# The 3x3 convolution of an image moved into the next image's attention stretch, and its last norm and routing moved behind that image's Gelu

## The chip, the core and the metric

The kernel runs on one core of a Trainium2 chip. The metric is the device time in microseconds of one execution. The engines are PE (TensorE, matrix products), DVE (VectorE), ACT (ScalarE), POOL (GpSimd) and SP (SyncE, which issues most DMAs). Each takes its instructions in the order in which the program lists them, and an instruction that waits holds up all those behind it on its engine.

## The reference

Four images of 256 channels and 32 x 32 = 1024 positions, all in float32. Each image goes through a mixing network and then, as 1024 tokens, through a mixture of eight experts of which each token takes two:

```python
xm = mamba_v(xc, ...) + skip_scale * xc              # 4 selective scans over 1024 steps
g  = sigmoid(conv1d(conv1d(x_concat, ...)))          # gates
R  = conv1d(conv1d(xg, ...)) + xg                    # depthwise and pointwise
xm2 = conv1d(conv1d(cat, ...)) + cat[:, :C]
x_local  = conv1d(xm2, lc_w, ...)                    # depthwise
x_global = mha(xm2, ...)                             # 8 heads over 1024 positions
x_out = gelu(layernorm(concat(x_local, x_global) @ fc_w.T + fc_b))
xi = conv3x3_depthwise(ln_hw(x_out))                 # norm over positions, then 3 x 3
x  = x + layernorm(xi) @ proj_w.T + proj_b
# experts, per token
top_w, top_i = top_k(layernorm(t) @ Wg + bg, 2)
t = t + sum_of_two(softmax(top_w) * (gelu(t_n @ W1[e] + b1[e]) @ W2[e] + b2[e]))
```

## The kernel before, in words

**Work pieces.** Every piece of an image's work is a Python generator that emits instructions and yields a number of ticks. `scan(at, i, stop)` emits one step of the selective scan; an image has eight parts (four scans of two halves) of 16 steps. A step is, on DVE, the product dBu (L538, into PSUM) and the scan hs (L545); on ACT the decay dA (L531); on POOL hs times cs (L550) and, in first halves, a copy of the last column (L549); on PE the sums of states yp (L556) and the spread bs (L523). A part ends with `finish_part` or its like inside the next part: yp, the gather on DVE (L563), a product on POOL (L566), the output matmul op on PE (L571), the skip on DVE (L577).

**The order.** It is written by hand. `beat()` advances a tick and lets every running generator that is due emit its next instructions. The main loop calls one scan step and one beat in turn, so background pieces are laced between scan steps. For image b > 0:

- with part 0, `convolutions(b - 1)` starts (gates, depthwise and pointwise convolutions, then the values, queries and keys of attention);
- after part 3, `drain()` runs all background to its end, and the attention stretch begins: `attention(b - 1)` followed by `mixing(b - 1)`, `finish_part`, `local(b - 1)` (the depthwise convolution into xloc) and `normalised(b + 1)` (the first norm of the next image: mean and variance matmuls on PE, L343; DVE L396 and L418; POOL L406, L416, L421);
- no scan step is emitted until attention has three of its 32 steps left; then parts 4 to 7 of image b run, with the rest of attention and `mixing(b - 1)` in the background.

An attention step (`logits`, then the products with the values) is 4 products st on PE (L861), 4 exponentials on ACT (L871), 4 products av (L903); every second step DVE adds the exponentials in pairs (L913), which the sums with a matrix of ones on PE read a step later (L881). DVE scales a finished block (L893).

**`mixing(b)`** is one generator: the output product of attention (ao) and the joint product (fc), on PE with ACT evictions; a norm over channels (squares on ACT, `column_mean` on PE, `root` on ACT, a product on DVE, L987); Gelu (L993); then statistics over positions (L1005, L1006), the image normed and padded by windows (xz, L1022), the centre tap (L1027, ACT) and eight further taps per half of the channels on DVE (L1035: 16 an image); then the last norm (mean matmuls, centring L1045, squares, variance, root, product L987), the projection (pr, added to the input xr, L1062) and `experts.dispatch`: 16 transposes (raw, L1428), statistics (L1438), gate products, the two best experts, places by counts, and 16 indirect DMAs on POOL (L1539), each preceded by a memset (L1538), which scatter the rows to the experts' regions in DRAM.

**The tail.** After the last scan, `finish_part`, `convolutions(3)` and `tiles()` run together. `tiles()` multiplies blocks of 256 rows of one expert: SP loads the weights (2 MB) and the rows (xs), PE transposes the rows (xp, L1734), 16 products h (L1757) with Gelu on ACT (L1762), 16 products y (L1767), DVE adds the bias and weighs, POOL adds the rows to the output by indirect DMA (L1778). The tiles come in series of 8, 8 and 23, of which the last four are done only if needed: series 0 needs the rows of images 0 and 1, series 1 those of image 2, series 2 those of image 3. Tiles are held while `attention(3)` runs, and go on beside `mixing(3)`, at a rate that `PACE` sets. Last, `bring_back` transposes the result to the output.

**Buffers.** Tiles of an image's size lie in a pool of eight (`a8`), those of half that in a pool of seven (`a4`), rows of 512 in a pool of 17 (`a2`); PSUM has eight banks.

Of the kernel before, what the change touches and what calls it, by code (L numbers as in the profile page):

```python
# [16 lines left out]
NC2 = C // P  # L17
# [54 lines left out]
def network(  # L72
# [70 lines left out]
    with tc.tile_pool(name="w_conv", bufs=1) as wp, tc.tile_pool(  # L143
# [789 lines left out]
            del XM2[b]  # L933


        def mixing(b):

            xloc, oT = XLOC.pop(b), OT.pop(b)
            xglo = a8(f"xglo_{b}")

            def pace(ticks):

                if b == B - 1:
                    T["pace",] = ticks

            pace(PACE["product"])
            yield from in_turn(
                CO_H, lambda at: product(
                    f"ao_{b}_{at[0]}_{at[1]}", aoutT_s, at[0],
                    [oT[ci][:, half(at[1])] for ci in range(NC2)],  # L950
                ),
                lambda at, r: nc.scalar.activation(
                    xglo[:, at[0], half(at[1])], r, AF.Identity, bias=ob[:, at[0] : at[0] + 1]
                ),
            )

            xc = a8(f"xc_{b}")
            both = (xloc, xglo)
# [10 lines left out]
            def inverse_deviation(name):  # L969
                r = a4(f"r_{name}")  # L970

                def squares(h):
                    sq = [a2(f"sq_{name}_{h}_{c}") for c in range(NC2)]
                    for c in range(NC2):
                        nc.scalar.activation(sq[c], xc[:, c, half(h)], AF.Square)
                    return sq

                for h in range(2):
                    sq = squares(h)
                    yield 1  # L980
                    var = column_mean(f"var_{name}_{h}", sq)
                    yield 2
                    root(r[:, half(h)], var, eps5)
                    yield 1
                yield 1
                for c in range(NC2):
                    nc.vector.tensor_tensor(xc[:, c, :], xc[:, c, :], r, ALU.mult)  # L987
                    yield 1

            pace(PACE["norm"])  # L990
            yield from inverse_deviation(f"lgn_{b}")
            for c in range(NC2):
                nc.scalar.activation(  # L993
                    xc[:, c, :], xc[:, c, :], AF.Gelu, bias=col("lgn_b", c), scale=col("lgn_w", c)
                )
            loaded[0] = None
            log_exp()
            yield 2


            mv = small.tile([P, NC2, 2], F32, tag="mv", name=f"mv_{b}")
            for c in range(NC2):
                st = small.tile([P, 2, 6], F32, tag="bn", name=f"bn_{b}_{c}", bufs=2)
                for h in range(2):
                    nc.vector.bn_stats(st[:, h, :], xc[:, c, half(h)])  # L1005
                nc.vector.bn_aggr(mv[:, c, :], st.rearrange("p a b -> p (a b)"))  # L1006
                yield 1
            rs = small.tile([P, NC2, 2], F32, tag="rs", name=f"rs_{b}")
            root(rs[:, :, 0:1], mv[:, :, 1:2], eps5)
            yield 1  # L1010
            nc.vector.scalar_tensor_tensor(
                rs[:, :, 1:2], mv[:, :, 0:1], -1.0, rs[:, :, 0:1], ALU.mult, ALU.mult
            )
            yield 1
            xi = a8(f"xi_{b}")
            xz = []
            pace(PACE["taps"])
            for c in range(NC2):
                xz.append(
                    act4.tile([P, HH, WW], F32, tag="a4", name=f"xz_{b}_{c}")  # L1020
                )
                nc.scalar.activation(  # L1022
                    xz[c].rearrange("p i j -> p (i j)"), xc[:, c, :], AF.Identity,
                    bias=rs[:, c, 1:2], scale=rs[:, c, 0:1],
                )

                nc.scalar.activation(  # L1027
                    xi[:, c, :], xz[c].rearrange("p i j -> p (i j)"), AF.Identity,
                    bias=col("dwc_b", c), scale=col("dwc_w", 9 * c + 4),
                )  # L1030
                yield 1
                for k in (0, 1, 2, 3, 5, 6, 7, 8):
                    acc = xi[:, c, :].rearrange("p (i j) -> p i j", j=WW)
                    (to_i, at_i), (to_j, at_j) = (edge(d - 1) for d in divmod(k, 3))
                    nc.vector.scalar_tensor_tensor(  # L1035
                        acc[:, to_i, to_j], xz[c][:, at_i, at_j], col("dwc_w", 9 * c + k),
                        acc[:, to_i, to_j], ALU.mult, ALU.add,
                    )
                    yield 1 if k % 2 else 0

            xc = xi

            def centre(h, mean):
                for c in range(NC2):
                    nc.vector.tensor_tensor(  # L1045
                        xc[:, c, half(h)], xc[:, c, half(h)], mean, ALU.subtract
                    )

            pace(PACE["norm"])
# [7 lines left out]
            yield from inverse_deviation(f"fin_{b}")  # L1057
# [14 lines left out]
            pace(PACE["rows"])  # L1072
# [5 lines left out]
            pace(1)  # L1078


        def tiles():
# [100 lines left out]
        def one_by_one(*what):  # L1182
            for w in what:
                yield from w

        def flagged(what, *flag):
            yield from what
            T[flag] = True
# [11 lines left out]
        with tc.manual_schedule(engines=ALL):  # L1200
# [4 lines left out]
            for b in range(B):  # L1205
                for p in range(PARTS):
                    at = b * PARTS + p
                    stop = b > 0 and p == PARTS // 2 - 1 or at == len(parts) - 1
                    if b == 0 and p == 2:
                        start(normalised(1))  # L1210
                    if b > 0 and p == 0:
                        start(convolutions(b - 1))
                    if at == len(parts) - 1:
                        start(tiles())
                    for i in range(NSTEP):
                        scan(at, i, stop)
# [689 lines left out]
```

## Time and profile before

| | |
|---|---|
| median of 3 runs | 2511.09 us (2509.42 to 2511.86) |
| profiled execution | 2513.66 us, of which the span from first to last instruction is 2511.8 us |
| busy over the span | PE 85%, DVE 65%, ACT 47%, POOL 46% |
| first scan begins, last scan ends | 81.2 us, 1723.35 us |
| attention stretches (no scan on DVE) | 535.7 to 633.0, 996.0 to 1093.3, 1456.4 to 1541.8 us |
| granted PE clock, mean | 0.903 |

Times in rows are microseconds from the span's start. A row of the windows has, for a stretch, its length and then each engine's busy time with the number of instructions, the granted clock of PE, the busy share of the DMA engines and what they moved. PE counts two records for each float32 matmul. "<-" names what an engine waited for. Busy shares are averages over stages with different limits, so they are read by stretch.

### The profile page before, as it was taken

What the parts mean: (1) busy time and instruction counts of PE and PEld (TensorE: products, weight loads), DVE (VectorE), ACT (ScalarE), POOL (GpSimd) and SP (SyncE); (2) the same over time, 40 slices, a digit from 0 to 9 for tenths busy, and PEclk for the clock granted to TensorE, in tenths of its full rate; (3) what the DMA queues carried; (4) which work ended last, traced back from release to release, by engine and by line L of the source; (5) the groups of instructions that cost most, each with busy time, mean ns of one, the idle gap of its engine ahead of it and who ended that gap; (6) DMA issues with size and microseconds to landing.
All of it is one profiled execution on the core that took longest, in us unless ns stands there. A gap on an engine that the chain in (4) does not pass through costs nothing. (4 is left out here: it accounts for less than half of the span.)

```text
span 2511.8 us, 28315 instructions
## 1 busy us (share of the span) xinstructions
PE 2124.0 (85%) x8810; PEld 945.7 (38%) x8810; DVE 1632.1 (65%) x2243; ACT 1192.2 (47%) x2014; POOL 1160.5 (46%) x1163
## 2 busy tenths in 40 slices
PE   5776778899977879997786999758899999699995
PEld 2111111333312213331221322214674366588884
DVE  2688898875799997578999766897324434311111
ACT  1544455368645534776444478632325853222221
POOL 2577777541576595146758613663421011322221
PEclk8788897899978879998787999979999999899997
DMA  3443342320233233022342210333443034666664
GB/s 94 98 112 96 85 117 70 73 68 26 51 89 98 72 102 89 9 59 65 85 110 85 66 42 22 81 108 123 142 112 89 1 93 143 192 194 193 193 197 147
DMA packets 154540, 244.17 MB, mean 97 GB/s; under 512 B 34016, under 2 KB 103300, under 8 KB 154376
## 3 DMA queue, kind: packets, MB, share of 16 engines
q1 hardware_dynamic: 133856, 215.46, 30.4%
q0 software_dynamic: 13744, 19.31, 3.8%
q10 hardware_dynamic: 6776, 7.45, 0.9%
q8 instruction: 74, 1.21, 0.2%
q14 instruction: 90, 0.74, 0.1%
HBM read 141.16 MB, written 33.85 MB: 70 GB/s over the span
## 5 line engine op out<-in xcount | busy, mean ns | idle before, releaser
L550 POOL TENSOR_TENSOR hs<-hs,cs 128x512 f32<-128x512 f32 x512 | 687.6, 1344 | 215.7 <-DVE hs L545 160.0
L531 ACT ACTIVATE dA<-dts,A 128x512 f32<-128x512 f32 x512 | 344.5, 715 | 285.2 <-DMA dts<-dt 191.0
L556 PE MATMUL yp<-hs,quads 128*32 128x512 f32 x1024 | 317.4, 677 | 162.2 <-POOL hs L550 124.0
L538 DVE TENSOR_TENSOR dBu<-dts,bs 128x512 f32<-128x512 f32 x512 | 348.6, 681 | 67.3 <-DMA dts<-dt 24.2
L1778 POOL DMA_INDIRECT Y<-ys,dest x70 | 113.5, 1622 | 582.2 <-DVE ys L1777 430.6
L545 DVE TENSOR_TENSOR_SCAN hs<-dA,last,dBu 128x512 f32<-128x512 f32 x256 | 327.7, 1280 | 24.6 <-DVE dBu L538 0.5
L545 DVE TENSOR_TENSOR_SCAN hs<-dA,dBu 128x512 f32<-128x512 f32 x256 | 312.5, 1221 | 33.5 <-ACT dA L531 8.6
L1762 ACT ACTIVATE hs<-h,b 128x256 f32<-128x256 f32 x280 | 117.2, 472 | 425.9 <-PE h L1757 222.0
L871 ACT ACTIVATE e<-st 128x512 f32<-128x512 f32 x512 | 263.4, 605 | 94.9 <-PE st L861 94.5
L1767 PE MATMUL y<-w,hs 128*128 128x256 f32 x1120 | 263.8, 388 | 8.9 <-ACT hs L1762 8.9
L1757 PE MATMUL h<-xT,w 128*128 128x256 f32 x1120 | 252.6, 381 | 0.0
L549 POOL COPY last<-hs 128x1 f32<-128x1 f32 x256 | 92.5, 361 | 311.8 <-DVE hs L545 305.1
L1767 PEld LDWEIGHTS y<-w,hs 128*128 128x128 f32 x1120 | 215.0, 195 | 46.8 <-ACT hs L1762 11.0
L913 DVE TENSOR_TENSOR e<-e,e 128x512 f32<-128x512 f32 x256 | 177.0, 753 | 79.1 <-PE av L903 61.6
L1757 PEld LDWEIGHTS h<-xT,w 128*128 128x128 f32 x1120 | 212.5, 191 | 40.6 <-issue 9.7
L1735 DVE COPY xT<-xp 128x512 f32<-128x512 f32 x35 | 24.2, 691 | 303.5 <-PE xp L1734 292.9
L523 PE MATMUL bs<-u,xpwT_s 128*32 128x512 f32 x1024 | 181.0, 677 | 35.1 <-DVE hs L545 29.9
L556 PEld LDWEIGHTS yp<-hs,quads 128*32 128x32 f32 x1024 | 52.9, 119 | 389.2 <-POOL hs L550 263.6
L861 PE MATMUL st<-qk 32*128 32x512 f32 x1024 | 188.5, 647 | 4.7 <-DVE hs L545 4.5
L439 PE MATMUL up<-xn,inwk 64*128 64x512 f32 x256 | 149.0, 733 | 18.4 <-DVE hs L545 12.3
L903 PE MATMUL av<-e,v 128*32 128x512 f32 x1024 | 141.1, 615 | 0.0
L861 PEld LDWEIGHTS st<-qk 32*128 32x128 f32 x1024 | 67.0, 185 | 125.5 <-issue 81.0
(271 smaller groups left out, 2522.9 us busy)
## 6 DMA issues: line engine op xcount, KB each, us to landing
w<-in_W_dram SPq DMA_DIRECT2D x136, 512.0 KB
dts<-dt SPq DMA_DIRECT2D x512, 128.0 KB
cs<-cd SPq DMA_DIRECT2D x512, 64.0 KB
xs<-XS SPq DMA_DIRECT2D x35, 260.0 KB
b<-in_b_dram SPq DMA_DIRECT2D x35, 128.0 KB
xn<-in_x_dram SPq DMA_DIRECT2D x4, 1024.0 KB
XL<-xl SPq DMA_DIRECT2D x8, 512.0 KB
xl<-XL SPq DMA_DIRECT2D x4, 1024.0 KB
```

What stands on the lines that cost most here:

```text
L439: nc.tensor.matmul(up, inwk[rows, c, k, :], XN[b][rows, c, ds(k + h * HALF, HALF)], start=(k == 0), stop=(k == KC - 1),)
L523: nc.tensor.matmul(bs[r], xpwT_s[:, n, s : s + 1].to_broadcast([P, 32]), T[b, n, "u"][:, half(h)], start=True, stop=True,)
L531: nc.scalar.activation(dA, T[b, n, h, "dts", g][:, 0, :], AF.Exp, scale=A[:, g, n, q : q + 1])
L538: nc.vector.tensor_tensor(dBu, T[b, n, h, "dts", g][:, 1, :], T[b, n, h, "bs", q], ALU.mult)
L545: nc.vector.tensor_tensor_scan(hs, T[b, n, h, "dA", i], dBu, 0.0 if h == 0 else last, ALU.mult, ALU.add)
L550: nc.gpsimd.tensor_tensor(hs, hs, T[b, n, h, "cs", q], ALU.mult)
L556: nc.tensor.matmul(T[b, n, h, "yp"][ts(g, 32)], quads, T[b, n, h, "hs", q * GD + g], start=(q == 0), stop=(q == GS - 1),)
L861: nc.tensor.matmul(sts[i], k[r, ts(kt, P)], q[r, half(h)], start=True, stop=not shifted)
L871: nc.scalar.activation(es[i], sts[i], AF.Exp, scale=1.0 / HD**0.5)
L913: nc.vector.tensor_tensor(first[i], first[i], es[i], ALU.add)
L1757: nc.tensor.matmul(hp[:, i, :], w1(c, k), xT[:, c, :], start=(c == 0), stop=(c == NC2 - 1))
L1767: nc.tensor.matmul(yp[:, ts(t, C)], hs[:, k, ts(t, P)], w2(k), start=(k == 0), stop=(k == NHC - 1))
```

## The change

`mixing` is cut into three generators: `joined` (ao, fc, the norm over channels, Gelu), `around` (statistics over positions, xz, the taps) and `sent_off` (last norm, projection, dispatch). The image between them is kept in `XC[b]`, one tile of the pool of eight. In the attention stretch of image b - 1, `around(b - 2)` runs behind `local(b - 1)`, so for images 0 and 1 a whole image later than before. `sent_off(b - 2)` starts when `joined(b - 1)` sets a flag: "joining" (fc is emitted) in the stretch that attends image 1, "attending" (its start) in the one that attends image 2. `normalised(3)` no longer starts with the attention stretch but behind `around(0)`. Image 2's `around` and `sent_off` start with `convolutions(3)` at the beginning of the tail. Image 3 goes through the three in a row, as before. `pace` and `inverse_deviation` become functions of their own with the image and the tile as arguments.

```diff
+        XC = {}
+
+        def pace(b, ticks):
+
+            if b == B - 1:
+                T["pace",] = ticks
...
-        def mixing(b):
+        def joined(b):
 
             xloc, oT = XLOC.pop(b), OT.pop(b)
+            pace(b, PACE["product"])
             xglo = a8(f"xglo_{b}")
...
+            T["attending", b] = True
...
-            xc = a8(f"xc_{b}")
+            xc = XC[b] = a8(f"xc_{b}")
...
+            T["joining", b] = True
+            pace(b, PACE["norm"])
+            yield from inverse_deviation(f"lgn_{b}", xc)
...
+        def around(b):
+
+            xc = XC.pop(b)
             mv = small.tile([P, NC2, 2], F32, tag="mv", name=f"mv_{b}")
...
-            xi = a8(f"xi_{b}")
+            xi = XC[b] = a8(f"xi_{b}")
...
-            xc = xi
+        def sent_off(b):
+
+            xc = XC.pop(b)
...
+        def behind_flag(flag, what):
+            while not T.get(flag):
+                yield 1
+            yield from what
...
                     if b > 0 and p == PARTS // 2 - 1:
                         drain()
-                        behind_ = [attention(b - 1), mixing(b - 1)]
-                        start(one_by_one(*behind_), finish_part(at), local(b - 1))
-                        if b + 1 < B:
+                        start(
+                            one_by_one(attention(b - 1), joined(b - 1)), finish_part(at),
+                            one_by_one(
+                                local(b - 1), *([around(b - 2)] if b > 1 else []),
+                                *([normalised(b + 1)] if 1 < b < B - 1 else []),
+                            ),
+                        )
+                        if b > 1:
+                            flag = "attending" if b == B - 1 else "joining"
+                            start(behind_flag((flag, b - 1), sent_off(b - 2)))
+                        if b == 1:
                             start(normalised(b + 1))
...
             start(
                 flagged(finish_part(len(parts) - 1), "whole", B - 1),
                 flagged(convolutions(B - 1), "convolved"),
+                one_by_one(around(B - 2), sent_off(B - 2)),
             )
...
-            start(mixing(B - 1))
+            start(one_by_one(joined(B - 1), around(B - 1), sent_off(B - 1)))
             drain()
```

More of the change, by code (lines that the diff above doesn't have):

```diff
@@ L933, in local, with inverse_deviation, squares @@
             del XM2[b]
-        def mixing(b):
+        XC = {}
+        def pace(b, ticks):
+            if b == B - 1:
+                T["pace",] = ticks
+        def inverse_deviation(name, xc):
+            r = a4(f"r_{name}")
+            def squares(h):
+                sq = [a2(f"sq_{name}_{h}_{c}") for c in range(NC2)]
+                for c in range(NC2):
+                    nc.scalar.activation(sq[c], xc[:, c, half(h)], AF.Square)
+                return sq
+            for h in range(2):
+                sq = squares(h)
+                yield 1
+                var = column_mean(f"var_{name}_{h}", sq)
+                yield 2
+                root(r[:, half(h)], var, eps5)
+                yield 1
+            yield 1
+            for c in range(NC2):
+                nc.vector.tensor_tensor(xc[:, c, :], xc[:, c, :], r, ALU.mult)
+                yield 1
+        def joined(b):
             xloc, oT = XLOC.pop(b), OT.pop(b)
+            pace(b, PACE["product"])
             xglo = a8(f"xglo_{b}")
[L941 to L946, printed above, removed]
+            T["attending", b] = True
             yield from in_turn(
@@ L967, in mixing @@
             )
[L969 to L991, printed above, removed]
+            T["joining", b] = True
+            pace(b, PACE["norm"])
+            yield from inverse_deviation(f"lgn_{b}", xc)
             for c in range(NC2):
@@ L1014, in mixing @@
             yield 1
-            xi = a8(f"xi_{b}")
+            xi = XC[b] = a8(f"xi_{b}")
             xz = []
-            pace(PACE["taps"])
+            pace(b, PACE["taps"])
             for c in range(NC2):
@@ L1047, in centre @@
                     )
-            pace(PACE["norm"])
+            pace(b, PACE["norm"])
             xr = a8(f"xr_{b}")
@@ L1056, in mixing @@
             )
-            yield from inverse_deviation(f"fin_{b}")
+            yield from inverse_deviation(f"fin_{b}", xc)
             def residual(at, r):
@@ L1071, in mixing @@
             )
-            pace(PACE["rows"])
+            pace(b, PACE["rows"])
             yield from experts.dispatch(
@@ L1077, in mixing @@
             T["sent", b] = True
-            pace(1)
+            pace(b, 1)
         def tiles():
@@ L1184, in one_by_one @@
                 yield from w
+        def behind_flag(flag, what):
+            while not T.get(flag):
+                yield 1
+            yield from what
         def flagged(what, *flag):
```

## The prediction

> **What bounds the kernel now.** I read the busy time by stretches first, cut where the scans of VectorE (DVE) show the stages: two stretches of scans (633 to 996 and 1093 to 1456, eight parts each), two attention stretches between them, the last four parts of scans, and the tail.
>
> ```profile
> core 0: us, PE busy (x) PEld busy (x) DVE busy (x) ACT busy (x) POOL busy (x), PEclk, DMA share, GB/s
> ...
> 633.00:996.00 363.00, 298.94 (x959) 91.66 (x958) 329.61 (x391) 185.33 (x279) 251.71 (x253) 0.85 0.32 83
> 996.00:1093.30 97.30, 97.27 (x622) 28.65 (x622) 57.59 (x76) 74.12 (x146) 15.98 (x11) 0.96 0.09 30
> 1093.30:1456.40 363.10, 295.18 (x959) 91.06 (x958) 328.06 (x391) 185.18 (x279) 250.91 (x253) 0.86 0.33 83
> 1456.40:1541.80 85.40, 85.32 (x606) 24.15 (x606) 47.35 (x71) 69.69 (x138) 2.93 (x2) 0.98 0.04 10
> 1541.80:1723.40 181.60, 128.13 (x419) 36.74 (x418) 162.83 (x198) 84.74 (x128) 116.41 (x106) 0.85 0.33 93
> 1723.40:2511.80 788.40, 720.02 (x3418) 532.31 (x3416) 232.67 (x584) 275.49 (x534) 157.59 (x146) 0.95 0.48 140
> ```
>
> Scans are bound by DVE (329.6 of 363 us). Attention is bound by PE (back to back), with DVE at 47.4 of 85.4. In the tail PE is busy 91% and DVE 30%. So the change takes DVE work out of the one place where DVE is late.
>
> Next, two stretches of the same four scan parts and the same convolutions, the first without the previous image's routing, the second with it:
>
> ```profile
> 365.40:535.70 170.30, 147.50 (x462) 45.85 (x462) 148.36 (x155) 88.30 (x129) 116.84 (x114) 0.87 0.32 81
> 807.60:996.00 188.40, 155.18 (x510) 50.31 (x510) 170.99 (x217) 90.00 (x134) 132.03 (x146) 0.86 0.33 88
> ```
>
> Routing costs 188.4 - 170.3 = 18.1 us there. Then the groups of the part that holds the taps (1620 to 1670):
>
> ```profile
> L1035 DVE SCALAR_TENSOR_TENSOR xi<-xz,V,xi 128x961 f32<-128x961 f32 (+1 forms) x16 | 20.5, 1281 | 0.2
> ```
>
> Sixteen taps, 20.5 us, and no idle around them: paid in full. Last, PE's order of time in the tail, where it idles for tile rows:
>
> ```profile
> 1912.04 1.12 PE L1734 MATMUL xp<-ident,xs 128*128 128x128 f32 x4 [5.33 <-DMA xs<-XS]
> ...
> 2194.80 1.11 PE L1734 MATMUL xp<-ident,xs 128*128 128x128 f32 x4 [19.36 <-DMA xs<-XS]
> ```
>
> **The change, stretch by stretch.** Nothing is computed less. I call the moved pieces *around* (taps and statistics) and *sent off* (norm, projection, routing). Around costs DVE 20.5 + 4 x 0.672 (L1005) + 2 x 0.209 (L1006) = 23.6 us. Sent off costs 4 x 0.672 (L1045) + 2 x 1.206 (L987) + 4 x 0.732 (L1062) = 8.0, and the routing 18.1: 26.1.
>
> *633 to 996*: image 0's around and sent off both leave: -23.6 - 26.1 = -49.7. Should the 3.1 us of statistics only uncover a wait of the join ahead of them, -46.6. I take -48.
>
> *996 to 1093 (attention of image 1)*: two things. The norm of image 3 now stands behind around. This stretch has it and the next has not: 97.3 - 85.4 = 11.9 us is its price. In the built order its four mean matmuls still fall in here (8 records x 0.593 = 4.7), the rest not: -7.2. Around of image 0 comes in. In the order of time two attention steps take 5.2 us on PE (the sums of L881 start at 1493.52 and 1498.72), in which DVE's four adds take 2.5. The built order puts 4, 3, 3, 3 and 3 taps behind five groups of adds: 5 x 2.5 + 20.5 + 0.7 (one L893) = 33.7 us of DVE against 5 x 5.2 = 26.0 of PE. The adds feed matmuls (L881) that PE takes in order; today they end at 1496.3 and the sums start at 1498.7, some 2 us early. So PE waits 33.7 - 26.0 - 2 = 5.7; I take 5.5. The bounds are 0 (the queue gives way) and 12.7: the full 7.7, and the 5.0 of ACT's four passes (L1022, L1027, 1.24 each) queued ahead of the exponentials. Sum: -1.7.
>
> *1093 to 1456*: image 1's around leaves, -23.6. Its sent off leaves as image 0's comes: 0. The rest of image 3's norm comes: 2 x 1.483 (L418) = 3.0 on DVE, and four variance matmuls, 4.8 on PE, in the part where PE joins attention and projections. The 16 indirect DMAs (L1539) now stand in POOL's queue beside bare scan steps: 1.34 (L550) + 0.18 (half of L549's 0.36) + 1.11 + 0.15 (L1538) = 2.8 us a step against DVE's 0.68 + 1.25 = 1.9, so over 16 steps POOL falls up to 14 us behind, and PE's sums with it. The third part of an image, by its scans, took 52.5 with such DMAs (image 2) and 50.2 without (image 1); I take 4, twice that. Sum -11.8, between -20.6 and -1.8.
>
> *1456 to 1542 (attention of image 2)*: around of image 1 alone, +5.5, between 0 and 12.7.
>
> *1542 to 1723*: around of image 2 and the 8.0 leave (its routing was in the tail already); image 1's whole sent off comes: -31.6 + 26.1 = -5.5. It starts with the join, where the built order has eight more matmuls among PE's projections, 9.6 us, and the dBu products wait for PSUM banks that these hold (L538 waits 18.4 us for fc's evictions, L964, over the span now). I take 6 of that: +0.5, between -5.5 and +10.
>
> *Tail*: PE bounds it, so PE's work counts. It gains 16 matmuls (mean, var, pr) x 2 x 0.593 = 19.0, six transposes of routing and four of tile 0, 10 x 0.29 = 2.9: +21.9. Before, tile 0 ran from 1721.8, ahead of the last scan's end at 1723.35; now its transposes stand behind the last op (L571, ends 7.6 us after the scan), of which PE itself works 2.1: +5.5. The mean matmuls wait for the last tap: DVE has 2.6 (until the gather L563) + 0.7 + 23.6 + 5.1 (first taps of image 3's convolutions) + some 3 of tiles = 35 us before that, PE 7.6 + 14.2 (a tile) + 14.2 (L701) + 2.3 (transposes) = 38, a tie; +3 for it. There are two more table loads on ACT between tile Gelus: +2.6. In return two waits close. Only seven tiles, not eight, run ahead of attention 3, so tile 8's rows are long there: -5.3. And a whole tile more (14.2 us apart) stands between image 3's last indirect DMA and the tile that waited 19.4 for it; two more output DMAs of 1.6 in POOL's queue push back: -12.5. Sum +15.2, between +4 (nothing exposed) and +33 (neither wait closes).
>
> The sum is -48 - 1.7 - 11.8 + 5.5 + 0.5 + 15.2 = -40.3. The profiled execution took 2513.66 (span 2511.8), 2.6 above the median of 2511.09. So 2513.7 - 40.3 = 2473.4, and against the median 2471.
>
> **Two rules beside rows.** Beside taps, POOL slows:
>
> ```profile
> 1666.77 1.09 POOL L549 COPY last<-hs 128x1 f32<-128x1 f32 x1 [0.87 <-DVE hs L545]
> ...
> 1669.81 0.18 POOL L549 COPY last<-hs 128x1 f32<-128x1 f32 x1 [0.60 <-DVE hs L545]
> ```
>
> The same copy takes 1.09 us while taps run and 0.18 after the last. The Trainium skill ("SBUF — State Buffer", "Who interferes with whom") makes the port that the two share an exclusive lock, taken by a DVE operation with two SBUF inputs. By the rule the scans gain a little more than DVE's 23.6 where POOL is the late one; I add nothing, since POOL is busy only 251.7 of 363. A rule that speaks against the change is about tables:
>
> ```profile
> 1749.03 1.28 ACT L321 ACT_TABLE_LOAD   x1
> 1750.32 0.30 ACT L327 ACTIVATE r<-mv,eps 128x8 f32<-128x8 f32 x1
> ```
>
> The next activation starts 0.01 us after the load, so a switch costs 1.3 here. The skill ("ScalarE: Activation LUTs", "What ACT_TABLE_LOAD costs") adds a drain and comes to 2.66 us. By it the two loads would be 5.3 and the sum 2.7 worse; the row shows no drain, and the row decides.
>
> **The rivals.** (a) *Slower.* DVE takes its queue in order, and what waits behind taps is what PE needs (adds, xT, the centred image). If around is uncovered in all three new places, it costs 23.6 in each: 2 x (23.6 - 5.5) + (23.6 - 3) = 56.8 more, 2528. It decides once the five groups of adds lose more than the idle between them. Against it: in the attention stretch DVE idles 38 of 85 us, half of it ahead of these very adds, as the waits of 1460 to 1540 say:
>
> ```profile
> DVE e L913 <- PE av L903: 18.4, 9, 2.7
> ```
> (b) *POOL takes the place of DVE* in the scans: in two bare parts of image 0 (300.1 to 365.4) POOL is busy 50.6 us and DVE 61.7, and routing's DMAs add some 20 to POOL in one burst. Then 633 to 996 gives 30 and the next nothing: 18 + 11.8 = 29.8 back, 2501. For it: PE already waits for POOL beside the taps; against it: those waits go with the taps. (c) *The tail's waits stay*: the rows of series 2 come as late after the last tile as now, since POOL's own chain sets them. 5.3 + 12.5 back: 2489. That the change does not do what it says I exclude: in the built order all taps of images 0 and 1 stand between attention's adds.
>
> **How the numbers follow.** The forecast has 0.70, (b) 0.12, (c) 0.13, (a) 0.05. A difference under 0.2% (5 us) is about what a measurement of this kernel can't tell from none. Faster 0.93, same 0.02 (between (b) and (a)), slower 0.05. The terms' ends do not fall together: half of their better ends gives 2453, and the upper end takes in (c) and reaches to (b): 2452 to 2500.
>
> **What would show it.** Right: parts 6 and 7 of image 1 last about 33 us each (54 and 38 now); the attention stretches last about 96 and 91; the scans end near 1668; the tail lasts about 803, and PE's wait ahead of tile 16's transposes is under 8 us. Wrong: attention stretches over 105 and 98 (rival a), POOL named ahead of PE's sums through bare parts (b), a wait of 19 us in the tail (c).

## The result, and the profile after

The changed kernel takes 2482.29 us (median of 4 runs, 2479.75 to 2486.92); the kernel before took 2511.48 beside it. The ratio is 0.9883, with a 95% interval from 0.9862 to 0.9904, so 29 us are gained. The profiled execution took 2486.92 us, with a span of 2485.2.

The windows of the changed kernel, cut at the same places as those of before (the columns are the same):

```profile
core 0: us, PE busy (x) PEld busy (x) DVE busy (x) ACT busy (x) POOL busy (x), PEclk, DMA share, GB/s
628.50:944.20 315.70, 268.88 (x875) 77.75 (x874) 277.00 (x296) 172.40 (x258) 218.29 (x220) 0.91 0.33 82
944.20:1040.00 95.80, 94.69 (x614) 26.74 (x614) 71.60 (x98) 74.66 (x144) 3.03 (x3) 0.95 0.07 20
1040.00:1398.50 358.50, 295.75 (x967) 91.42 (x966) 308.74 (x370) 184.93 (x281) 249.57 (x261) 0.86 0.33 87
1398.50:1490.90 92.40, 91.33 (x606) 26.00 (x606) 69.19 (x93) 74.50 (x144) 2.93 (x2) 0.95 0.07 21
1490.90:1678.40 187.50, 142.22 (x455) 41.23 (x454) 159.59 (x232) 80.95 (x128) 113.51 (x135) 0.83 0.29 80
1678.40:2485.20 806.80, 736.18 (x3465) 538.68 (x3464) 262.36 (x621) 289.07 (x551) 160.69 (x151) 0.96 0.48 143
```

| stretch | before | after | moved by | predicted |
|---|---|---|---|---|
| up to the first attention's end (code unchanged) | 633.0 | 628.5 | -4.5 | 0 |
| scans beside image 0's join | 363.0 | 315.7 | -47.3 | -48 |
| attention of image 1 | 97.3 | 95.8 | -1.5 | -1.7 |
| scans beside image 1's join | 363.1 | 358.5 | -4.6 | -11.8 |
| attention of image 2 | 85.4 | 92.4 | +7.0 | +5.5 |
| last four scan parts | 181.6 | 187.5 | +5.9 | +0.5 |
| tail | 788.4 | 806.8 | +18.4 | +15.2 |

The first row differs in code that the change doesn't touch. In the other runs image 0's scans alone lasted 281 to 289 us, so some 4 us of any single comparison are of this kind. Without that row the stretches moved by -22.1, where -40.3 was forecast; the medians, over several executions each, say -29. Later stretches agree better between runs of the same code: the attention stretches and the last four parts within 1.5 us, the scans beside image 1's join within 5.

Where the gain was made, the four scan parts that carried image 0's routing are now as long as the same four parts of the image before, which never had any:

```profile
360.90:531.20 170.30, 147.68 (x462) 45.91 (x462) 148.31 (x155) 88.15 (x129) 116.65 (x114) 0.87 0.32 81
773.90:944.20 170.30, 147.79 (x462) 45.91 (x462) 148.29 (x155) 88.29 (x129) 116.65 (x114) 0.87 0.32 81
```

The taps now stand in the attention stretch. By the groups of VectorE in the one that attends image 1, they last about as long as before (19.7 us for 20.5) and wait for next to nothing, and 6.6 us of waiting ahead of the adds (L913) are left:

```profile
L913 DVE TENSOR_TENSOR e<-e,e 128x512 f32<-128x512 f32 x60 | 38.4, 702 | 6.6 <-PE av L903 6.6
L1040 DVE SCALAR_TENSOR_TENSOR xi<-xz,V,xi 128x992 f32<-128x992 f32 x8 | 10.0, 1252 | 0.2
L1040 DVE SCALAR_TENSOR_TENSOR xi<-xz,V,xi 128x961 f32<-128x961 f32 x8 | 9.7, 1217 | 1.3 <-ACT xi L1032 1.2
```

The tail multiplies one tile of 256 rows after another; I number them from 0. PE's order of time has tile 8's transposes without a wait (5.33 before), but tile 16's with a longer one (19.36 before):

```profile
1996.94 0.60 PE L1755 MATMUL xp<-ident,xs 128*128 128x128 f32 x4
...
2167.15 1.12 PE L1755 MATMUL xp<-ident,xs 128*128 128x128 f32 x4 [22.40 <-DMA xs<-XS]
```

### The profile page after: what moved, and what is told of

Its sections match the earlier page's. It is cut to its first block, busy times and chain, and to the rows that moved or that the text cites. A ratio compares the mean times of both kernels' runs of the same rounds, so it can differ in the third digit from the quotient of the medians.

```text
span 2485.2 us, 28288 instructions
## 1 busy us (share of the span) xinstructions
PE 2122.3 (85%) x8810; PEld 941.7 (38%) x8810; DVE 1622.3 (65%) x2243; ACT 1193.9 (48%) x2016; POOL 1111.8 (45%) x1163
## 5 line engine op out<-in xcount | busy, mean ns | idle before, releaser
L550 POOL TENSOR_TENSOR hs<-hs,cs 128x512 f32<-128x512 f32 x512 | 669.5, 1309 | 222.0 <-DVE hs L545 175.1
L556 PE MATMUL yp<-hs,quads 128*32 128x512 f32 x1024 | 344.5, 684 | 173.1 <-POOL hs L550 123.2
L1788 PE MATMUL y<-w,hs 128*128 128x256 f32 x1120 | 259.6, 383 | 4.8 <-ACT hs L1783 4.8
L1788 PEld LDWEIGHTS y<-w,hs 128*128 128x128 f32 x1120 | 212.2, 192 | 43.4 <-issue 10.1
L523 PE MATMUL bs<-u,xpwT_s 128*32 128x512 f32 x1024 | 176.9, 670 | 40.6 <-DVE hs L545 23.6
L549 POOL COPY last<-hs 128x1 f32<-128x1 f32 x256 | 66.3, 259 | 318.0 <-DVE hs L545 309.5
L913 DVE TENSOR_TENSOR e<-e,e 128x512 f32<-128x512 f32 x256 | 171.4, 732 | 53.9 <-PE av L903 44.0
L861 PE MATMUL st<-qk 32*128 32x512 f32 x1024 | 194.0, 655 | 6.8 <-DVE hs L545 4.5
L439 PE MATMUL up<-xn,inwk 64*128 64x512 f32 x256 | 131.7, 659 | 15.6 <-DVE hs L545 9.2
```

The source lines that it names most:

```text
L523: nc.tensor.matmul(bs[r], xpwT_s[:, n, s : s + 1].to_broadcast([P, 32]), T[b, n, "u"][:, half(h)], start=True, stop=True,)
L550: nc.gpsimd.tensor_tensor(hs, hs, T[b, n, h, "cs", q], ALU.mult)
L556: nc.tensor.matmul(T[b, n, h, "yp"][ts(g, 32)], quads, T[b, n, h, "hs", q * GD + g], start=(q == 0), stop=(q == GS - 1),)
L861: nc.tensor.matmul(sts[i], k[r, ts(kt, P)], q[r, half(h)], start=True, stop=not shifted)
L913: nc.vector.tensor_tensor(first[i], first[i], es[i], ALU.add)
L1788: nc.tensor.matmul(yp[:, ts(t, C)], hs[:, k, ts(t, P)], w2(k), start=(k == 0), stop=(k == NHC - 1))
```

## The experiments

Four questions were open: what taps cost beside scans, what made the attention stretches longer, why tile 16 still waits, and what the later scans lost.

### What the taps cost beside scans

`before_no_taps` is the kernel before without the eight shifted taps of images 0 to 2:

```diff
-  nc.vector.scalar_tensor_tensor(acc[...], xz[c][...], ...)      # kernel before
+  if b > 2: nc.vector.scalar_tensor_tensor(acc[...], xz[c][...], ...)
```

> The kernel before without the eight shifted taps per half of the channels (L1035) of images 0, 1 and 2, all of which it has beside scan steps; the yields stay. The routing of these images sees other rows. Theory (scans are bound by DVE there, so the taps are paid in full, 20.5 us an image): the seventh part of images 1, 2 and 3 falls from 54 to about 33 us, the total by about 61. Rival 1 (POOL takes DVE's place as soon as the taps are gone): the parts fall by only 8 to 14 and the total by 24 to 42. Rival 2 (the port that DVE and POOL share was the price, and POOL's own steps get shorter too): the parts fall by more than 20.5.

The seventh parts last 33.4, 34.3 and 33.7 us (53.4 to 53.5 before): 19.2 to 20.0 less. So the taps were paid nearly in full. Over the whole stretches it was 17.7, 16.8 and 20.1, since the third parts of images 2 and 3, which hold some of the indirect DMAs, grew by 2.4 and 2.5. Why they grew isn't settled; a change of this size needs no cause in the edit, since image 1's third part lasts 47.7 to 50.3 us in runs that don't differ up to there. The whole time, 2488.13 us in one run, can't be compared: with other rows to route the tail ran 36 tiles and not 35 (1152 records of L1757's kind for 1120), as in the two runs below that leave taps out. POOL's groups in image 3's seventh part, first of the kernel before, then without taps:

```profile
L550 POOL TENSOR_TENSOR hs<-hs,cs 128x512 f32<-128x512 f32 x17 | 27.7, 1629 | 3.4 <-DVE hs L545 2.1
L549 POOL COPY last<-hs 128x1 f32<-128x1 f32 x16 | 12.1, 758 | 11.1 <-DVE hs L545 8.8 <-PE yp L556 1.6 <-DVE rs L1011 0.6
```

```profile
L550 POOL TENSOR_TENSOR hs<-hs,cs 128x512 f32<-128x512 f32 x17 | 21.6, 1270 | 3.4 <-DVE hs L545 2.1
L549 POOL COPY last<-hs 128x1 f32<-128x1 f32 x16 | 3.0, 185 | 6.7 <-DVE hs L545 6.1 <-DVE rs L1011 0.6
```

With only the taps gone, the same copies take 185 ns and not 758, the same products 1270 and not 1629. That is the price for POOL of the port that the prediction named, 15.2 us in these two groups. The part fell by the taps' own time and no more, so POOL's loss was hidden there.

### What made the attention stretches longer

`no_taps` is the changed kernel without those of images 0 and 1:

```diff
-  nc.vector.scalar_tensor_tensor(acc[...], xz[c][...], ...)      # changed kernel: no_taps
+  if b > 1: nc.vector.scalar_tensor_tensor(acc[...], xz[c][...], ...)
```

> The changed kernel without the eight shifted taps per half of the channels (L1040) of images 0 and 1, which it puts into the attention stretches; the yields stay, so everything else is emitted in the same order. The routing of these images therefore sees other rows. Theory (the taps are mostly covered by DVE's idle time, and what they cost is a queue ahead of the adds of the exponentials, about 5.5 to 7 us a stretch): the attention stretches fall from 95.8 to about 90 and from 92.4 to about 86, the four scan parts behind each are unchanged, the total falls by 11 to 14. Rival 1 (the stretch grew because of ACT's four passes, L1022 and L1027 as they were numbered before, or because of PE's own work): both stretches stay within 2 us. Rival 2 (the taps are not covered): each stretch falls by about 20.

```profile
1399.10:1491.50 92.40, 91.33 (x606) 25.75 (x606) 50.23 (x78) 74.47 (x144) 2.93 (x2) 0.94 0.07 21
```

The window of image 2's attention: VectorE has 19 us less to do, and the stretch is as long as with the taps (the other one 95.7). The theory, that the taps' queue ahead of the adds is the price, falls here; the first rival stands. So the passes of ScalarE (xz and the centre tap) were taken off its queue:

```diff
-  nc.scalar.activation(xz..., xc..., AF.Identity, bias=rs[...], scale=rs[...])   # acts_dve
-  nc.scalar.activation(xi..., xz..., AF.Identity, bias=dwc_b, scale=dwc_w)
+  nc.vector.tensor_scalar(xz..., xc..., rs[0:1], rs[1:2], ALU.mult, ALU.add)     # for b < 2
+  nc.vector.tensor_scalar(xi..., xz..., dwc_w, dwc_b, ALU.mult, ALU.add)
```

> The changed kernel, with the four passes of ScalarE of images 0 and 1 (normed image xz, L1027, and centre tap, L1032; 1.24 us each) done by VectorE instead, in the same places of the order. Theory (the attention stretches lost what they lost because these passes, 5.0 us, stand ahead of the exponentials that the matrix unit waits for; the taps on VectorE cost nothing there): the stretch that attends image 2 falls from 92.4 to 85.5 to 87, that of image 1 from 95.8 to 89 to 91, although VectorE gets some 5 us more; the total falls by 11 to 14. Rival 1 (the order of the statistics and the two square roots, or PE's own pace, set the length): no change within 2 us. Rival 2 (VectorE's queue was close to being late with the adds of the exponentials, and the passes push it over): the stretches stay or grow by 2 to 5 us.

Image 2's stretch stays at 92.4. Image 1's falls to 94.5, which is no gain: PE was granted 0.72 of its clock in the first 6 us of it and 0.50 in the changed kernel, and was 1.6 us ahead there already. The time is 2486.67 us (8 runs, 2476.21 to 2495.34), ratio to before 0.9924 [0.9898, 0.9951], no gain over the changed kernel. By the expectation this was the second rival: VectorE's queue now is too long. PE's order of time shows what took the place of what. First the changed kernel, where PE stops for the exponentials behind ScalarE's passes, then the one with the passes on VectorE, where the sums (L881) stop for the adds:

```profile
1455.52 1.51 PE L861 MATMUL st<-qk 32*128 32x512 f32 x4
1458.08 1.61 PE L861 MATMUL st<-qk 32*128 32x512 f32 x4 [1.04 <-ACT e L871]
```

```profile
1447.55 1.06 PE L903 MATMUL av<-e,v 128*32 128x512 f32 x8
1450.02 2.85 PE L881 MATMUL av<-e,every 128*32 128x512 f32 x8 [1.40 <-DVE e L913]
```

Much of such a delay is not in the brackets: a group of matmuls that lasts 2.85 us and not 1.04 waited inside itself. Both causes were then removed together (`neither`: the two edits above in one kernel).

> The changed kernel with both at once of what had no effect singly: the eight shifted taps per half of the channels of images 0 and 1 are left out, and their four passes of ScalarE (xz, L1027, and centre tap, L1032) are done by VectorE, 0.81 us each. The routing of these images sees other rows. Theory (two queues of nearly the same length stand ahead of the matrix unit, each of which hides the other: ScalarE's passes ahead of the exponentials, VectorE's taps ahead of their adds): the stretch that attends image 2 falls from 92.4 to 86 to 87.5, that of image 1 from 95.8 to 88.5 to 91. Rival (neither counts, and the length comes from the clock at the start, the square roots, or something not yet named): 91 or more for the stretch of image 2.

```profile
1385.00:1472.10 87.10, 87.10 (x608) 25.07 (x606) 53.23 (x83) 70.15 (x140) 2.92 (x2) 0.97 0.08 22
```

87.1, as the theory of two queues has it, and 89.3 for image 1's (1.6 of its 6.5 by the clock of the first 6 us, 0.72 again). The table has PE's lag behind the kernel before in image 2's stretch, by the starts of the same matmuls, in us:

| | after 11 us | after the two roots | after the first passes | after the second passes | at the end |
|---|---|---|---|---|---|
| changed kernel | 1.1 | 1.8 | 2.9 | 6.9 | 7.0 |
| no taps | 1.2 | 1.9 | 3.0 | 7.0 | 7.0 |
| passes on VectorE | 1.1 | 1.8 | 1.8 | 5.2 | 7.0 |
| neither | 1.0 | 1.7 | 1.7 | 1.7 | 1.7 |

So of the 7.0 us, 1.1 came in the first 6 us (where PE was granted 0.50 of its clock and 0.72 before), 0.7 with the two roots on ScalarE (L327, L328), and 5.1 with its four passes, 5.0 us of work. The 1.1 needs no cause in the change: the kernel before without taps, whose code in this stretch is that of the kernel before, was granted 0.50 there too and lagged 1.2 to the end (86.6).

With the passes on VectorE, its queue of taps and passes costs 5.3 over `neither`. That run put 3.2 us of passes into the queue; but in the changed kernel, too, VectorE's queue stands behind ScalarE's. The adds behind its last taps end at 1474.68, just as PE comes to their sums, and PE is 6.9 us late by then:

```profile
1472.19 2.49 DVE L913 TENSOR_TENSOR e<-e,e 128x512 f32<-128x512 f32 x4
...
1474.60 1.19 PE L881 MATMUL av<-e,every 128*32 128x512 f32 x8
```

The two queues stand side by side and not one behind the other: while PE waits for ScalarE, VectorE catches up. How long the queue of the taps alone would be was not run. It is no longer than 5.3, and my estimate from these rows is at least 3: had PE come 5.1 earlier (1469.5), and had VectorE not waited the 2.1 us that it does wait from 1440 on, these adds would have ended at 1472.6.

`one_tap` puts one tap, not two, into a tick, and the statistics beside the depthwise convolution:

```diff
-  yield 1 if k % 2 else 0
+  yield 1 if k % 2 or b < B - 2 else 0
```

> The changed kernel with the taps of images 0 and 1 one per tick instead of two, so two and not three or four behind each group of adds, and their statistics beside the depthwise convolution, one group earlier; four taps of image 1 fall into the scans. ScalarE's passes stay. Theory (two queues that hide each other): with the passes on ScalarE the stretch that attends image 2 stays at 91 to 93; that of image 1 falls by some 4 because the norm of image 3 moves on into the scans, which get that back. Rival (the taps' queue alone sets the length): image 2's stretch falls to 86 to 88.

Image 2's stretch is 93.6, not shorter, so ScalarE's passes alone hold it, as the theory had it; it is 0.6 above the range, because PE lagged 1.1 us more than in the changed kernel once the statistics, now ahead of the first adds, were through. Image 1's stays at 95.4 (4 less expected): the norm of image 3 left it, but PE lagged 1.4 us behind the changed kernel after the statistics, and 3.0 after the second passes. The total was 2491.67 us in one run. No tap fell into the scans.

### Why tile 16 still waits

The wait is put down to the rows' DMA. But POOL's and SP's order of time in the changed kernel show that the last row left at 2142.78, and that SP turned to this tile's weights and rows only at 2155.84, after the table of series 2:

```profile
2142.78 0.96 POOL L1560 DMA_INDIRECT XS<-XR,to  x1 [0.19 <-issue]
2144.04 1.61 POOL L1799 DMA_INDIRECT Y<-ys,dest  x1 [0.30 <-issue]
2148.62 1.56 POOL L1799 DMA_INDIRECT Y<-ys,dest  x1 [2.97 <-issue]
2149.63 0.86 POOL L1582 IOTA steps<- 128x128 f32 x1
```

```profile
2155.84 0.97 SPq L1735 DMA_DIRECT2D w<-in_W_dram  x2
...
2160.64 0.38 SPq L1709 DMA_DIRECT2D xs<-XS  x1
```

The table begins with a step of POOL (steps, L1582), which the program emits with the first load of series 2, behind an output DMA of tile 14. It says where the tiles' rows lie, and needs only the counts. The edit (`table_early`) emits it as soon as image 3 is counted:

```diff
+  if len(tables) == 2 and experts.counted == B - 1:
+      table(2)
```

> The changed kernel, with the table of the tiles of series 2 (the steps of GpSimd and VectorE that turn counts into regions, and what SP loads weights and rows by) emitted as soon as the rows of image 3 are counted, ahead of its 16 indirect DMAs, and not after the last tile of series 1. Theory (in the changed kernel the wait of 22.4 us ahead of the transposes of tile 16 is the wait for this table, which stands behind the output DMAs of tile 14 in GpSimd's queue, and no longer the wait for the rows): the wait falls to 5 to 8 us and the total by 14 to 17. Rival (the rows of image 3, that is GpSimd's chain of indirect DMAs and what follows it, set the time, as in my case c): the wait stays at 19 or more and the total within 3 us; a smaller fall of 4 to 8 would mean that both come late and the rows are next.

```profile
2130.39 0.60 PE L1760 MATMUL xp<-ident,xs 128*128 128x128 f32 x4
...
2148.84 0.60 PE L1760 MATMUL xp<-ident,xs 128*128 128x128 f32 x4
```

PE's rows of tiles 15 and 16 have no wait left (5 to 8 expected). They are 18.5 us apart and not 36.8 (later tiles 14.25). The tail lasts 790.7, 16.1 less than in the changed kernel; the time is 2465.83 us (4 runs, 2461.00 to 2470.75), ratio 0.9838 [0.9798, 0.9878]. That interval overlaps the changed kernel's; the tail tells more, since it lasts 806.8 to 809.5 in the four runs that differ only ahead of it. The rows would have been there. In the kernel before it was the other way round: the table's step ran at 2172.43, the last row left only at 2188.00, and SP loaded the rows at 2192.09.

The other question of the tail is what image 2's piece costs there. `tail_back` puts it back into the scans:

> The changed kernel, with image 2's convolution, last norm, projection and routing back in a row behind its join, beside the scans, as before, and only images 0 and 1 put into the next attention stretch. Theory (terms of the prediction: PE is the bound in the tail, and the work is dearer in the scans, where VectorE pays 23.6 + 8.0 for it): the last four scan parts grow by 25 to 32, the tail falls by 12 to 18, the total rises by 10 to 17. Rival (the tail's loss comes from the late table of series 2, whose place does not depend on image 2's routing): the tail falls by less than 8 and the total rises by 20 or more.

```diff
-  one_by_one(attention(b - 1), joined(b - 1))
+  one_by_one(attention(b - 1), joined(b - 1), *([around(b - 1), sent_off(b - 1)] if b == B - 1 else []))
```

With image 2's piece back, the last scan parts grow by 30.0 (217.5) and the tail falls by 21.9 (784.9; 12 to 18 expected). By these two stretches the kernel is 8 us slower than the changed one (2491.83 us in one run), a little less than expected, because the tail fell by more. The tail of this run, and its wait for tile 16:

```profile
1705.20:2490.10 784.90, 721.72 (x3427) 533.34 (x3426) 235.59 (x590) 276.29 (x535) 156.24 (x148) 0.96 0.51 146
```

```profile
PE xp L1757 <- DMA xs<-XS: 17.0, 1, 17.0
```

PE is busy 14.5 us less than in the changed kernel's tail (736.18) and idle 7.4 less; 5.4 of that is tile 16's wait (17.0 for 22.4). So moving image 2 gained 30 in the scans and lost 22 in the tail, two thirds of it PE's own work. That the prediction also had 21.9, for PE's work alone, is chance.

### What the later scans lost

`ind_spread` issues image 0's indirect DMAs every second beat:

```diff
-  self.sent.append(ins); yield 1
+  self.sent.append(ins); yield 2 if b == 0 else 1
```

> The changed kernel, with the 16 indirect DMAs of image 0 (the burst in the last part of image 2's scans and the first of image 3's) issued every second beat instead of every beat. Theory (in the burst GpSimd needs about 2.5 to 3 us a step against DVE's 1.9, and the matrix unit's sums wait for it; spread over twice as many steps GpSimd stays below DVE): the two parts of 52 us become about 46 to 49 each, the stretch of 358.4 loses 4 to 8 us. Rival (the parts are long because DVE and PE have the join's and the norms' work there): the stretch stays within 2 us; if the delay only pushes the DMAs into the following parts, the sum of the four parts of image 3 grows by what the first two lose.

With the gaps behind them, the two parts of 52.1 and 52.2 became 52.1 and 42.6, the next grew from 44.5 to 48.0, and the stretch lasts 352.3: 6.1 less. That is one pair of profiles. In all the runs, these three parts together last 144.3 to 148.8 us without the gaps (8 runs) and 142.2 to 143.3 with them (4 runs), so the gaps gain 1 to 7. The whole time shows no gain over the changed kernel (2477.23 us, ratio 0.9888 [0.9848, 0.9928]). The theory holds, but only for one of the two parts. PE's waits over both parts, changed kernel and then this one:

```profile
PE yp L556 <- POOL apart L1559: 14.1, 9, 2.8
...
PE yp L556 <- POOL hs L550: 2.3, 1, 2.3
```

```profile
PE yp L556 <- POOL hs L550: 6.6, 5, 2.3
...
PE yp L556 <- POOL apart L1559: 5.7, 3, 3.6
```

The sums' wait for POOL's memsets between the DMAs fell from 14.1 to 5.7; that for POOL's products rose from 2.3 to 6.6, so for POOL altogether it fell by 4.1. The eighth part of image 2 stays: from 1162 to 1220 us VectorE is busy 54.9 of 58 in both kernels, with the routing's small steps among the scans.

`later_1` asks why the last four parts grew:

```diff
-  flag = "attending" if b == B - 1 else "joining"
+  flag = "joining"
```

> The changed kernel, with the last norm, projection and routing of image 1 started when the joint product of image 2 is emitted (the flag joining, as for image 0) and not at the beginning of its join. Theory (the first two of the last four scan parts grew from 82.6 to 95.2 us because the matrix unit has 32 more records of mean, variance and projection there, 15.3 us, besides the join): the first part falls from 48.3 to about 43.5 and PE's busy time in it by about 5 us; the work comes back in the second and third part, where PE has room, so the first three fall from 145.3 to 136 to 141; against it, the last indirect DMAs fall behind the scans, and the tail, whose first tile waits for them, grows by 5 to 15. Rival (VectorE's own moved work, 8 us of norm and some routing, made these parts long): the first three parts together stay within 2 us.

The windows of the first two of the last four parts, before, changed, and with image 1 sent off later:

```profile
1541.80:1624.40 82.60, 72.02 (x253) 21.41 (x252) 69.78 (x80) 53.70 (x84) 51.28 (x53) 0.96 0.30 75
```

```profile
1490.90:1586.10 95.20, 86.54 (x305) 29.06 (x308) 77.62 (x95) 59.49 (x94) 52.75 (x53) 0.96 0.26 65
```

```profile
1495.00:1580.90 85.90, 77.39 (x266) 24.63 (x266) 71.91 (x79) 57.33 (x90) 52.74 (x53) 0.95 0.33 83
```

PE gained 14.5 us of work there and the parts 12.6; with the work moved on, the first part is 43.5 again and the first three 124.5, further down than expected. The edit moves VectorE's part of the work too (77.62 us busy and then 71.91), so it doesn't tell PE's from VectorE's; PE, busy 86.5 of 95.2 us, is the fuller one. The last part grew to 59.8, the stretch lost only 3.1, and the tail grew by 34.6 (5 to 15 expected); of PE's waits there, the one of the mean matmuls for taps (L343) grew from 0.7 to 14.0 and that of the products y (L1788) from 4.8 to 15.4, the rest was not traced. 2522.39 us in one run: the early start is right. What the projection (pr) costs PE in the changed kernel's two parts:

```profile
L334 PE MATMUL pr<-xi,projT_s 128*128 128x512 f32 x16 | 7.6, 605 | 0.0
```

Each record lasts 605 ns, but sixteen of them take 7.6 us and not 9.7, because they overlap.

### Together

`combo` has the early table, image 0's spread DMAs and the passes on VectorE.

> The changed kernel with three edits together: the table of series 2 ahead of image 3's indirect DMAs, the indirect DMAs of image 0 every second beat, and the four passes of ScalarE of images 0 and 1 on VectorE. If the three causes are separate, their gains add: about 14 to 16 (tail) + 6 (scans of image 3's first half) + 11 to 14 (attention), so 2445 to 2453 against 2482 of the changed kernel, ratio to before 0.974 to 0.978. If they are one and the same wait, the sum is less than 25.

2464.09 us (4 runs), ratio 0.9820 [0.9778, 0.9862]. The scans' stretch lasts 350.7 and the tail 792.8, as hoped, but the attention stretches 95.8 and 91.3 (what 91.3 is below 92.4 is the clock, 0.72 in the first 6 us): the gain expected there was the one that one of two queues doesn't give. The next two also shorten the taps' queue: `v3d` adds the edit of `one_tap`, `final` only the one tap a tick, for image 1 alone.

> Four edits on the changed kernel: the table of series 2 ahead of image 3's indirect DMAs; the indirect DMAs of image 0 every second beat; the four passes of images 0 and 1 on VectorE; and their taps one per tick, with the statistics beside the depthwise convolution. Theory (both queues gone at once): the stretch that attends image 2 falls from 92.4 to 86 to 88, that of image 1 from 95.8 to 85.5 to 89 with up to 4 of that back in the scans of image 3's first half, the tail stays near 791, and the time is 2446 to 2456, that is 10 to 18 below the same kernel with its taps as they were (2464). Rival (no second queue, the stretches have another bound): 2460 or more.

2459.70 us (5 runs, 2455.76 to 2467.86), ratio 0.9797 [0.9778, 0.9816]. The stretches of 89.7 and 89.6 are shorter, by less than hoped, and image 3's norm, pushed into the scans, takes 10 back and not up to 4 (360.7 against 350.7). So the time misses its range and all but reaches the rival's 2460, though the second queue is there.

> The three edits together (table of series 2 early, image 0's indirect DMAs every second beat, the passes of images 0 and 1 on VectorE), and the taps of image 1 alone one per tick, so two and not three or four behind each group of adds; statistics and the norm of image 3 stay where the changed kernel has them. Theory (with the passes off ScalarE, only the taps' queue is left, and two taps fit between two groups of adds): the stretch that attends image 2 falls from the 91.3 of the three edits alone to 87 to 88.5, all else as there (350.7 for image 3's first half, 187.4 for its last four parts, a tail near 792), a median of 2458 to 2463. Rival (the adds are late for another reason than the number of taps behind them): the stretch stays at 90.5 or more.

Image 2's stretch is 89.0, half a microsecond over its range, and 2.3 less than in `combo` at the same granted clock in its first 6 us; the scans are as expected. The tail is 798.7 and not 792: PE is busy 747.5 us there, and 738.7 in `combo` with the same matmuls, at a granted clock of 0.95 and 0.96. 2463.88 us (5 runs, 2456.16 to 2469.34), ratio 0.9819 [0.9795, 0.9843]. All three beat the kernel before, and by their ratios the changed one too, by 0.6 to 0.9% of the time before (the interval of `combo` just meets the changed kernel's); among themselves and against the early table alone (0.9838) the intervals overlap.

## Why the prediction was right, and where its steps were not

- **As a whole** the forecast was 2471 and the time is 2482.3: a gain of 29 for 40. Several of its terms are off by 5 us or more, and part of that cancels, which is luck.
- **Scans beside image 0's join** (-48 for -47.3): right, with its signs: parts 6 and 7 (the seventh and eighth) were predicted at 33 us each and last 32.0 and 33.7. The rival that POOL takes DVE's place was excluded here, as `before_no_taps` shows from the other side.
- **Attention** (-1.7 and +5.5 for -1.5 and +7.0, of which 1.1 is the clock): the sizes were right and the step behind them was not. "PE waits 33.7 - 26.0 - 2 = 5.7" was worked out for the taps; in the changed kernel taking the taps away gives nothing, and ScalarE's four passes cost 5.1. The 5.0 of the passes stood only in the upper bound, on top of the taps, as if the two queues added up. They overlap. That both are some 5 us long made the number come out.
- **Scans beside image 1's join** (-11.8 for -4.6): the -23.6 held; in image 0's stretch the two parts with the statistics and the taps fell by 25.0 (39.1 to 36.2 and 54.1 to 32.0). What was mis-sized is "Its sent off leaves as image 0's comes: 0", with the burst, "I take 4". Image 1's sent off, where it stood before, made the four parts around it 22.5 longer than the same parts without such work (33.7, 43.3, 44.2 and 50.3 in the changed kernel), and not 26.1. Image 0's, with the norm of image 3, now makes seven parts 42.9 longer (326.1 for 283.2), and not 3.0 + 4.8 + 26.1 + 4 = 37.9. The burst's share of it isn't settled: issuing it at half the rate gave back 1 to 7, and the 52.5 and 50.2 that the 4 was taken from differ by less than one such part does from run to run (47.7 to 50.3).
- **Last four parts** (+0.5 for +5.9, inside its bounds): "eight more matmuls, 9.6 us, I take 6" was mis-sized: mean, variance and projection are sixteen matmuls (32 records). In the two first parts PE had 14.5 us more to do, and the parts grew by 12.6.
- **Tail** (+15.2 for +18.4): the sum is near because its errors cancel. The step that failed is the -12.5: "a whole tile more stands between image 3's last indirect DMA and the tile that waited" is true of the rows, but when the rows came early the table was late, and the wait became 3.0 longer. (By its own terms, 14.2 - 2 x 1.6, the step gives 11.0.) Against it, PE's own work was put too high: 2 x 0.593 a matmul is the duration of its two records, which overlap. PE's busy time grew by 16.2 and not 21.9. Of the exposures (5.5, 3 and 2.6) some showed: PE waited 4.3 more until the last scan's output, and 3.7 for the squares of image 2's norm; for the mean matmuls it waited 0.7, as before, and its waits of the products y for Gelu fell by 4.1. The -5.3 came true.
- So the case with the tail's waits half came about, with its sign, a wait of 19 us or more, for another reason than it gave: the early table shows that not POOL's chain of rows set it. The wait was to be under 8 us and was 22.4. The scans were to end near 1668 and end at 1678.4; the tail lasts 806.8 and not 803.

## What to carry to other kernels

Work put into an engine's idle time is priced by every queue that it joins: here four cheap passes on one engine cost more than sixteen taps on another, and two such queues side by side hide each other: emptying one, or moving the other's work into it, showed nothing here, and only both together did. A wait that is named after a DMA may be a wait for what lets the DMA be issued: look at when the data was ready and when the issuing queue got to it. When an early step is moved, ask of each later one that was "early enough" if it still is. And a measured number that equals a term of the sum doesn't confirm it until busy time and waits are told apart: 21.9 here was 14.5 of work and 7.4 of waits.

## What the runs showed of the hardware

- The shared port of VectorE and GpSimd: with only the taps removed, POOL's copy of 128 x 1 fell from 758 to 185 ns and its 128 x 512 product from 1629 to 1270. The Trainium skill ("SBUF — State Buffer", "Who interferes with whom") says that a VectorE operation with two SBUF inputs contends with a GpSimd instruction that reads SBUF. The runs agree, and give the price.
- An affine pass over 128 x 1024 floats took 0.81 us on VectorE (TENSOR_SCALAR) where ScalarE took 1.23 to 1.30, and a tap over 128 x 961, with two tensors read, 1.22.
- A table load on ScalarE took 1.28 us in the changed kernel's tail too (at 1735.75), between activations that end at 1735.73 and start at 1737.04: no drain shows, as in the prediction's row.
- PE's granted clock in the first 6 us of image 2's attention was 0.72 before and 0.50 in the changed kernel, though PE had been busy 31 of the 32.5 us ahead in both; this alone was about 1.1 us. Code doesn't tell: the kernel before without taps had 0.50 in the same stretch, `combo` and `final` 0.72. What sets it was not tried.
